# Attention stage: reciprocal denominators carried through memory, a convolution tap on ScalarE and POOL, and new ranks in the plan

## The chip, the cores and the metric

The program runs on one core of one Trainium2 chip. A core has TensorE (PE, with its weight loads PEld), VectorE (DVE), ScalarE (ACT), GpSimd (POOL) and SyncE (SP, which here only issues transfers). The metric is the device time of one execution in microseconds; the median of three runs before the change is 3934.19 us.

## The reference

Two layers act on `x` of shape (32, 1024, 14, 14), in float32. Layer 0 (group normalisation and three table-lookup convolutions) is untouched by the change. Layer 1 is linear attention with a rotary embedding and a depthwise 3 x 3 convolution:

```python
q = elu(q_pre) + 1;  k = elu(k_pre) + 1            # q_pre, k_pre: 1x1 products over half of the channels each
q_rope, k_rope = rope(q), rope(k)
km = kh.mean(axis=-1)
z = 1.0 / (einsum('bhdn,bhd->bhn', qh, km) + 1e-06)
kv = s * s * einsum('bhdn,bhen->bhde', krh, vh)
out = einsum('bhdn,bhde->bhne', qrh, kv) * z[..., None]
lepe = conv_depthwise_3x3(x, lepe_w) + lepe_b
return attn + lepe                                  # x = x + layer1(group_norm(x))
```

There are 16 heads of 64 channels; an image has 196 positions.

## The kernel before, in words

Layer 0 runs first. When it is done, the attention stage handles 16 **pairs** of images, p = 0 to 15. Channels lie in 8 tiles of 128 partitions; a pair's tile has 2 x 196 = 392 columns. Each pair goes through these steps (the line is that of the instruction in the profile before):

- `load`: SP loads two halves h of four tiles into buffers `x` (L992) and the third convolution's output into `o3q` (L1006), two tiles at a time.
- `front`, `group_norm`, `normalise`: layer 0's last sum (L1023, L1032, L1037), statistics (L1042), averages on PE (L1064), `centred` and `variance` on DVE (L1072 to L1080), a power and small products on POOL (L238 to L1091), and two scaled copies by ACT (L1117): `y`, which is the attention's input with a border, and `x`, to which the middle tap of the convolution is already applied. `y` has two buffers, for even and odd pairs.
- `channels`: the query and key products, 4 matmuls each (L1149), relu and exp on ACT (L1158, L1161), and a maximum on DVE (L1166, L1170). A PE result takes one of 4 banks of the pool `mm`.
- `rope`: four products and sums on POOL for each of 4 key and 4 query tiles (L1190 to L1197).
- `v_tokens`, `k_tokens`, `products`: turns on PE (L1208) with copies by ACT (L1211), then kv on PE (L1245) and a mask on DVE (L1254).
- `normalisers`: means of k (L1278), denominators on PE (L1296), then `z`, the reciprocals, on DVE (L1305, L1306). `z` holds 4 rows in use for each group of 32 partitions.
- `normalise_q`, four times: a matmul with a selection matrix spreads the four rows over 128 partitions (L1317) into a bank of `mm`, ACT copies it into one of two buffers `zb` (L1323), and POOL multiplies the roped query `qr` by it (L1320).
- `attend`, four times, each for two tiles: the product of scaled query and kv into two of three banks `pa` (L1337).
- `lepe`, eight times: the other eight taps of the convolution, each one DVE instruction that adds a shifted and weighted `y` onto the bank (L1354), then the sum into `x` (L1368). `store` writes four tiles of `x` out (L1377).

No loop order sets where an instruction stands. Every step calls `do(engine, rank, weight, fn, reads, writes)`, which records a piece; `Plan.write` then plays all 16 pairs on paper, with the weights as durations. Each time an engine is free on paper, it is given the ready piece with the lowest rank for which buffers are free, and the real instruction is emitted then. On the chip each engine executes its own list in that order and waits where the real dependencies aren't met. A rank is a due time: pair p starts at t = 80 p, and `attend` and `lepe` of pair p have ranks over t + 80, so they stand among the work of pair p + 1. A piece's results count as there after its weight and a `lag` (0.12 for most).

Of the kernel before, what the change touches and what calls it, by code (L numbers as in the profile page):

```python
# [51 lines left out]
class Plan:  # L52
# [31 lines left out]
    def write(self):  # L84
# [29 lines left out]
        while events:  # L114
            now, _, done = heapq.heappop(events)
            if done is not None:
                for m in after[done]:
                    count[m] -= 1
                    if count[m] == 0:
                        heapq.heappush(ready[self.pieces[m][0]], (self.pieces[m][1], m))  # L120
                for s in self.pieces[done][5]:
                    s.left -= 1
            if events and events[0][0] <= now:
                continue
            for e in engines:
# [28 lines left out]
                heapq.heappush(events, (now + w, 2, None))  # L154
                heapq.heappush(events, (now + w + lag, 1, piece))
        assert left == 0, [p for p, c in zip(self.pieces, count) if c == 0][:0] or left
# [4 lines left out]
def conv_preact_kernel(ctx: ExitStack, tc: tile.TileContext, a: dict, out: bass.AP):  # L161
# [692 lines left out]
    with ExitStack() as s:  # L854
# [99 lines left out]
        bufs = dict(x=5, o3q=2, e=2, k=2, q=4, qr=5, ks=2, zb=2, mm=4, pa=3, w=1)  # L954
# [95 lines left out]
        def group_norm(p, h, rank):  # L1050
# [19 lines left out]
            def centred():  # L1070
                for t in (g("gd"), pd()):
                    nc.vector.tensor_tensor(t, mean, bc(pm()[:, :8], 2, 2), ALU.subtract)  # L1072
                nc.vector.tensor_tensor(g("gd"), g("gd"), pd(), ALU.mult)
                nc.vector.scalar_tensor_tensor(
                    g("gq"), m2, 1.0 / 98.0, g("gd"), ALU.mult, ALU.add
# [31 lines left out]
        def normalise(p, h, c, xt, rank):  # L1107
# [29 lines left out]
            do(ACT, rank + 24, 0.92, apply("xsc", "xbi", "x"), [key("xsc"), key("xbi")], [xk])  # L1137


        def channels(p, keys, j, r, t, sums, rank):  # L1140
# [35 lines left out]
            do(PE, rank, 2.76, product, ys_, [pq], lag=0.25)  # L1176
# [25 lines left out]
        def tokens(dst, dk, blocks, keys, rank):  # L1202
# [7 lines left out]
            do(PE, rank, 0.5, turn, keys, [pt], lag=0.25)  # L1210
# [12 lines left out]
        def k_tokens(p, i, h, jp, kt, rank):  # L1223
            tokens(
                lambda: kt()[:, jp],
                (kt, jp),
                lambda: [krs[2 * jp + j][:, r, i, h] for j in range(2) for r in range(2)],
                [("kr", 2 * jp + j) for j in range(2)],
                rank,
            )  # L1230
# [42 lines left out]
        def normalisers(qs, ks, rank):  # L1273
# [33 lines left out]

            qk = [(q, r) for q in qs for r in range(2)]
            do(PE, rank, 2.3, piece, [*qk, ("kmm", 0), ("kmm", 1)], [pd], lag=0.25)
            do(DVE, rank - 10, 3.0, inverse, [pd], ["z"])  # L1310

        def normalise_q(j, qr, rank):
            pz, zb = bank("mm"), slot("zb", [P, N2])
            v = slice(32 * j, 32 * j + 32)

            def spread():
                nc.tensor.matmul(pz()[:, :N2], sel[v], z[v], start=True, stop=True)  # L1317
# [4 lines left out]
            do(PE, rank, 0.6, spread, ["z"], [pz], lag=0.25)  # L1322
            do(ACT, rank - 10, 0.48, lambda: nc.scalar.copy(zb(), pz()[:, :N2]), [pz], [zb])  # L1323
            do(POOL, rank, 1.65, times, [zb], [qr], port=True)

        def attend(j, kvs, qr, rank):


            pa = [bank("pa") for hp in range(2)]
# [17 lines left out]

        def lepe(p, c, pa, xt, rank):


            def tap(k):
                def piece():
# [3 lines left out]
                        neighbours(p, c, 15 * (k // 3 - 1) + k % 3 - 1),  # L1356
# [13 lines left out]
            for n, k in enumerate([k for k in range(9) if k != 4]):  # L1370
# [14 lines left out]

        ru = once.tile([P, 2, N2], F32, tag="ru", name="ru")
        z = once.tile([P, N2], F32, tag="z", name="z")

        def pair(p, t):

            xts = {}
            for h in (1, 0):
                f = t - T + (20 if h else 50)
                xts[h], os = load(p, h, f)
                for c in range(4):
                    front(p, h, c, xts[h], os[c // 2], f + 6.5 * c)
                group_norm(p, h, f + 16)
                for c in range(4):
                    normalise(p, h, c, xts[h], f + 40 + c)
# [4 lines left out]
            for j in range(4):  # L1404
                k = slot("k", [P, 2, N2])
                for r in range(2):
                    channels(p, True, j, r, k, ks, t + 9 * j)
                kr = krs[j].rearrange("p r i h (n m) -> p (r i) (h n) m", m=15)[:, :, :, :14]
                rope(k, lambda kr=kr: kr, ("kr", j), j, t + 8 * j + 28)
            for j in range(4):  # L1410
                q, qr = slot("q", [P, 2, N2]), slot("qr", [P, 2, N2])
                for r in range(2):
                    channels(p, False, j, r, q, None, t + 22 + 8.0 * j + 3.0 * r)
                qv = lambda qr=qr: qr().rearrange("p r (i n m) -> p (r i) n m", i=2, m=14)
                rope(q, qv, qr, j, t + 34 + 9 * j + 26)
# [3 lines left out]
            for i in range(2):  # L1419
                for half in (1, 0):  # L1420
                    for h in range(2):
                        v_tokens(p, i, h, half, vts[i][h], t + (22 - 2.0 * half + 3 * h if i == 0 else 66 + h - 2 * half))
# [93 lines left out]
```

## Time and profile before

| | us |
|---|---|
| median of 3 runs (lowest, highest) | 3934.19 (3933.69, 3940.51) |
| the profiled execution, own time | 3939.01 |
| its span | 3937.2 |
| first product of the attention stage | about 2727 |
| start of the 1st, 15th and 16th reciprocal of `z` | 2789.7, 3805.6, 3876.4 |
| busy over the whole span: PE, DVE, POOL, ACT | 3750.7, 3058.5, 2225.9, 1705.0 |

The profile is of one execution. Its views used below are the table by windows (busy time of each engine in a stretch), the timeline of an engine (start, length, engine, line, operation, output and inputs, how many were merged, and in brackets the idle time before it and what ended it), the view of waits (who waited for whom: total us, times, longest), and the groups of instructions by line (busy us and mean ns of one). The mean of a group includes the part of an instruction that overlaps its successor. A matmul of float32 stands in the records as two rows, so one query or key product of 4 matmuls is 8 rows.

### The profile page before, as it was taken

Reading aid. Unit: us, or ns where it says so; the run is one execution under the profiler, and the core shown is the slowest. Engines: PE = TensorE matmul, PEld = TensorE weight load, DVE = VectorE, ACT = ScalarE, POOL = GpSimd, SP = SyncE. Lnnn points to the kernel's source line nnn. Section 1 sums busy time; section 2 is a strip of 40 time slices with the busy share of each in tenths; the row PEclk is TensorE's granted clock in tenths of the full one; section 3 lists DMA queues with packets and bytes.
Section 4 is the critical chain, followed back from the end, with each engine's and each line's share of the span. In section 5 each row is a group of like instructions: output and inputs, shape, how many; then the busy total and the mean of one; then the engine's idle time right before and its main releaser. Section 6 shows DMA issues by size and latency. Waiting matters only on the chain. (4 is left out here: it accounts for less than half of the span.)

```text
span 3937.2 us, 43888 instructions
## 1 busy us (share of the span) xinstructions
PE 3750.7 (95%) x15451; PEld 2172.6 (55%) x15451; DVE 3058.5 (78%) x4391; ACT 1705.0 (43%) x3797; POOL 2225.9 (57%) x1246
## 2 busy tenths in 40 slices
PE   8999999999999999999999999994999999999995
PEld 5555555545555555555444444442666666666664
DVE  8999999977888888888533333323799999999997
ACT  4554555533333333333222111213756666666661
POOL 7999999964444444444211111103877777777773
PEclk9999999998999999999999999997999999999997
DMA  3111111024454444544111100114122222222211
GB/s 113 33 34 33 33 33 33 1 65 83 74 70 72 69 66 71 73 71 64 38 38 38 38 26 31 38 38 135 42 63 66 70 70 64 64 70 69 60 54 33
DMA packets 202085, 220.19 MB, mean 56 GB/s; under 512 B 21048, under 2 KB 199736, under 8 KB 201856
## 3 DMA queue, kind: packets, MB, share of 16 engines
q1 hardware_dynamic: 201280, 217.15, 24.3%
q8 instruction: 124, 2.03, 0.2%
q14 instruction: 105, 0.86, 0.1%
q10 hardware_dynamic: 576, 0.15, 0.0%
HBM read 158.47 MB, written 58.79 MB: 55 GB/s over the span
## 5 line engine op out<-in xcount | busy, mean ns | idle before, releaser
L471 POOL TENSOR_TENSOR t<-t,r 128x1664 f32<-128x1664 f32 (+1 forms) x284 | 1063.9, 3746 | 1205.0 <-DVE r L470 1172.8
L504 PE MATMUL po<-t,lut 128*128 128x392 f32 x4096 | 1406.7, 497 | 0.5 <-POOL t L471 0.5
L504 PEld LDWEIGHTS po<-t,lut 128*128 128x128 f32 x4096 | 770.4, 190 | 594.0 <-issue 57.0
L433 ACT ACTIVATE t<-sc,cbias 128x392 f32<-128x392 f32 (+1 forms) x1136 | 620.6, 592 | 989.4 <-PE sc L722 584.7
L1149 PE MATMUL mm<-y,qk 128*128 128x392 f32 x2048 | 730.2, 509 | 4.1 <-POOL xbi L1091 4.1
L445 DVE STREAM_TRANSPOSE tt<-t 128x1664 f32<-128x1664 f32 (+1 forms) x284 | 544.5, 1917 | 183.0 <-ACT t L433 183.0
L808 PE MATMUL po<-t,lut 128*128 128x448 f32 x1792 | 680.3, 540 | 0.0
L1354 DVE SCALAR_TENSOR_TENSOR pa<-y,lepe_w,pa 128x406 f32<-128x406 f32 x1024 | 605.7, 635 | 10.5 <-PE pa L1337 9.3
L470 DVE STREAM_TRANSPOSE r<-rc 128x1664 f32<-128x1664 f32 (+1 forms) x284 | 546.6, 1925 | 20.6
L1149 PEld LDWEIGHTS mm<-y,qk 128*128 128x128 f32 x2048 | 387.8, 195 | 285.8 <-issue 36.2
L808 PEld LDWEIGHTS po<-t,lut 128*128 128x128 f32 x1792 | 338.4, 190 | 339.9 <-issue 339.6
L817 DVE BATCH_NORM_STATS2 stats<-o 128x6 f32<-128x448 f32 x112 | 68.9, 617 | 488.4 <-ACT o L816 488.4
L462 DVE TENSOR_REDUCE sm<-tt 128x104 f32<-128x832 f32 (+2 forms) x284 | 423.1, 1490 | 5.4
L722 PE MATMUL sc<-patch,cw 72*128 72x392 f32 x1024 | 365.8, 499 | 13.2 <-DMA patch<-h1d 10.1
L722 PEld LDWEIGHTS sc<-patch,cw 72*128 72x128 f32 x1024 | 195.8, 192 | 162.4 <-issue 21.5
L448 POOL TENSOR_TENSOR tt<-tt 128x832 f32<-128x832 f32 x128 | 247.9, 1937 | 7.8 <-DVE tt L445 7.8
L816 ACT COPY o<-po 128x448 f32<-128x448 f32 x112 | 59.0, 527 | 419.6 <-PE po L808 375.5
L464 DVE RECIPROCAL rc<-sm 128x104 f32<-128x104 f32 (+1 forms) x284 | 229.4, 808 | 9.8
L1190 POOL TENSOR_TENSOR kr<-k,cosq 128x784 f32<-128x784 f32 x64 | 104.1, 1627 | 132.8 <-DVE k L1170 107.4
L1320 POOL TENSOR_TENSOR qr<-qr,zb 128x784 f32<-128x784 f32 x64 | 116.0, 1844 | 103.7 <-ACT zb L1323 103.7
L472 ACT ACTIVATE sm<-sm 128x104 f32<-128x104 f32 (+1 forms) x284 | 82.9, 292 | 174.9 <-DVE rc L464 174.8
L1023 ACT ACTIVATE w<-x,tb,gn_a 128x196 f32<-128x196 f32 x256 | 133.3, 521 | 58.5 <-DMA x<-in_x_dram 34.0
(140 smaller groups left out, 3677.1 us busy)
## 6 DMA issues: line engine op xcount, KB each, us to landing
patch<-h1d SPq DMA_DIRECT2D x567, 108.5 KB
x<-in_x_dram SPq DMA_DIRECT2D x32, 784.0 KB
o3d<-o SPq DMA_DIRECT2D x14, 1792.0 KB
x<-in_x_dram SPq DMA_DIRECT2D x64, 392.0 KB
o3q<-o3d SPq DMA_DIRECT2D x64, 392.0 KB
out_dram<-x SPq DMA_DIRECT2D x64, 392.0 KB
lut<-in_lut_dram SPq DMA_DIRECT2D x24, 512.0 KB
h1d<-pad SPq DMA_DIRECT2D x32, 225.0 KB
```

What stands on the lines that cost most here:

```text
L433: nc.scalar.activation(t[:, j, : sc.shape[1]], sc, AF.Identity if exact else AF.Exp, bias=bias[:, j : j + 1],)
L445: nc.vector.transpose(tt, tf)
L448: nc.gpsimd.tensor_tensor(tv[:, :, :8], tv[:, :, :8], tv[:, :, 8:], ALU.add)
L462: nc.vector.tensor_reduce(sm, tv, AX.X, ALU.add)
L464: nc.vector.reciprocal(rc, sm)
L470: nc.vector.transpose(r, bc(rc, 2, KC))
L471: nc.gpsimd.tensor_tensor(tf, tf, r, ALU.mult)
L504: nc.tensor.matmul(po[h], luts[b][:, j, h * P : (h + 1) * P], ts[u % len(ts)][:, j, :N2], start=(b == 0 and j == 0), stop=(b == 7 and j == 3),
L722: nc.tensor.matmul(sc, w2[:, 4 * b + j, :], pv[:, 4 * (b % 2) + j, :, :14, :14], start=True, stop=True,)
L808: nc.tensor.matmul(po, luts[g][:, m * P : (m + 1) * P], t3[h][:, g % 4, :], start=(g == 0), stop=(g == 7),)
L1149: nc.tensor.matmul(pv(), w[kt][:, m0 : m0 + P], ywin(p, first + kt), start=(kt == 0), stop=(kt == 3),)
L1354: nc.vector.scalar_tensor_tensor(acc, neighbours(p, c, 15 * (k // 3 - 1) + k % 3 - 1), lw[:, c, k : k + 1], acc, ALU.mult, ALU.add,)
```

## The change

1. For pairs 0 to 14, `normalisers` writes `z` to a DRAM tile `zd` (two of them, for even and odd pairs) by a transfer on SP, and `normalise_q` reads each group's four rows back with a broadcast source, 32 times each, into one of now four buffers `zb`. The plan gives the write a lag of 2.5 and the reads of 5.0, 6.7, 8.4 and 10.1. Pair 15 keeps the matmul and the ACT copy.
2. In `lepe`, for tiles 4 to 7 one tap, and in pair 15 three taps of every tile, are taken from DVE: ACT multiplies the shifted window of `y` by the weight into a buffer `side` (of two), and POOL adds it onto `x`.
3. `centred` puts its squared difference into the bank and not into `gd`.
4. In the plan, a piece releases pieces of its own engine (other than SP) at once, without the lag. A key product of the next pair waits for the turns of this pair's keys (`held`), and a turn waits until its target buffer has room (`room`).
5. Nearly all ranks have new values, from a table `due`. In pair 15 the denominators have a lower rank, and every second `attend` takes its banks from `mm`.

The instructions of PE in steady pairs are the same apart from the spread's matmuls, which are left only in pair 15; their order changes. In a steady pair, PE has after the denominators: one turn, two key products of the next pair, two kv products, two more key products, an average of group normalisation, and then the first `attend`.

```diff
         while events:
-            now, _, done = heapq.heappop(events)
+            now, kind, done = heapq.heappop(events)
             if done is not None:
                 for m in after[done]:
-                    count[m] -= 1
-                    if count[m] == 0:
-                        heapq.heappush(ready[self.pieces[m][0]], (self.pieces[m][1], m))
-                for s in self.pieces[done][5]:
+                    own = self.pieces[m][0] == self.pieces[done][0] != "SP"
+                    if own == (kind == 0):
+                        count[m] -= 1
+                        if count[m] == 0:
+                            heapq.heappush(ready[self.pieces[m][0]], (self.pieces[m][1], m))
+                for s in self.pieces[done][5] if kind else ():
                     s.left -= 1
...
-                heapq.heappush(events, (now + w, 2, None))
+                heapq.heappush(events, (now + w, 0, piece))
                 heapq.heappush(events, (now + w + lag, 1, piece))
...
-        bufs = dict(x=5, o3q=2, e=2, k=2, q=4, qr=5, ks=2, zb=2, mm=4, pa=3, w=1)
+        bufs = dict(x=5, o3q=2, e=2, k=2, q=4, qr=5, ks=2, zb=4, side=2, mm=4, pa=3, w=1)
...
-                nc.vector.tensor_tensor(g("gd"), g("gd"), pd(), ALU.mult)
+                nc.vector.tensor_tensor(pd(), g("gd"), pd(), ALU.mult)
                 nc.vector.scalar_tensor_tensor(
-                    g("gq"), m2, 1.0 / 98.0, g("gd"), ALU.mult, ALU.add
+                    g("gq"), m2, 1.0 / 98.0, pd(), ALU.mult, ALU.add
                 )
...
-            do(PE, rank, 2.76, product, ys_, [pq], lag=0.25)
+            held = [("held", j // 2)] if keys else []
+            do(PE, rank, 2.76, product, ys_, [pq, *held], lag=0.25)
...
-            do(PE, rank, 0.5, turn, keys, [pt], lag=0.25)
+            do(PE, rank, 0.5, turn, keys, [pt, (dk[0], "room")], lag=0.25)
...
-                [("kr", 2 * jp + j) for j in range(2)],
+                [("kr", 2 * jp + j) for j in range(2)] + [("held", jp)],
...
+            def keep():
+                nc.sync.dma_start(zd[p % 2], z)
...
             do(DVE, rank - 10, 3.0, inverse, [pd], ["z"])
+            if p < NP - 1:
+                do(SP, rank - 10, 0.45, keep, ["z"], [("zd", p % 2)], lag=2.5)
...
             def spread():
+                nc.sync.dma_start(zb(), bc(zd[p % 2, 32 * j : 32 * j + 4], 1, 32))
+
+            def select():
                 nc.tensor.matmul(pz()[:, :N2], sel[v], z[v], start=True, stop=True)
...
-            do(PE, rank, 0.6, spread, ["z"], [pz], lag=0.25)
-            do(ACT, rank - 10, 0.48, lambda: nc.scalar.copy(zb(), pz()[:, :N2]), [pz], [zb])
+            if p < NP - 1:
+                do(SP, rank - 10, 0.58, spread, [("zd", p % 2)], [zb], lag=5.0 + 1.7 * n)
+            else:
+                do(PE, rank, 0.6, select, ["z"], [pz], lag=0.25)
+                do(ACT, rank - 10, 0.48, lambda: nc.scalar.copy(zb(), pz()[:, :N2]), [pz], [zb])
             do(POOL, rank, 1.65, times, [zb], [qr], port=True)
...
-            for n, k in enumerate([k for k in range(9) if k != 4]):
+            taps = [k for k in range(9) if k != 4]
+            last = p == NP - 1
+            shared = 3 if last else c // 4
...
+            def apart(k):
+                side = slot("side", [P, 2, 14, 14])
+
+                def shifted():
+                    nc.scalar.activation(
+                        side(), window(offset(k)), AF.Copy, scale=lw[:, c, k : k + 1]
+                    )
+
+                def onto():
+                    nc.gpsimd.tensor_tensor(
+                        xc(), xc(), side().rearrange("p i r c -> p (i r c)"), ALU.add
+                    )
+
+                do(ACT, rank - 6, 0.52, shifted, [("y", p % 2, c)], [side])
+                do(POOL, rank - 4, 1.02, onto, [side], [(xt, c % 4)], port=True)
+
+            for k in range(shared):
+                apart(taps.pop(1))
+            for n, k in enumerate(taps):
                 do(DVE, rank + n, 0.555, tap(k), [("y", p % 2, c)], [pa])
...
-            normalisers(qs, ks, t + 68)
+            normalisers(p, qs, ks, at["den"] - (10 if p == NP - 1 else 0))
...
+                pool = "mm" if p == NP - 1 and n % 2 else "pa"
+                pa = attend(j, kvs, qrs[j], pool, at["attend"] + due["sums"] * n)
```

Some of the new ranks, beside the old ones for a pair at t: the key product of tile j stood at t + 9 j and stands at t + 10.25 j; the denominators at t + 68, now t + 69; `normalise_q` at t + 70, now t + 64; `attend` number n at t + 82.5 + 19 n, now t + 82.5 + 20 n; the fronts of the halves began at t - 60 and t - 30 and begin at t - 72 and t - 28.

## The prediction

> **What bounds the kernel now.** The edits lie in the attention stage alone, so I read the tenths of part 2 only to place it (about 2697 us to the end) and then the stage by itself. First the table by windows, over twelve whole periods from one reciprocal to the same one twelve pairs on (2934.89 to 3805.60), with the columns PE, PEld, DVE, ACT, POOL, clock, DMA share, GB/s:
>
> ```profile
> 2934.89:3805.60 870.71, 856.24 (x5286) 578.04 (x5282) 833.72 (x1961) 570.60 (x1196) 642.02 (x576) 0.97 0.23 67
> ```
>
> Divided by 12: a pair takes 72.56 us, in which PE is busy 71.4, DVE 69.5, POOL 53.5, ACT 47.6. PE and DVE are both nearly full, and a busy PE here may be a PE that waits inside a group of matmuls. So next PE's timeline over a period, at the place where the reciprocal is used:
>
> ```profile
> 3589.64 2.39 PE L1317 MATMUL mm<-z,hsel 32*128 32x392 f32 x8 [0.99 <-DVE z L1306]
> 3591.96 7.23 PE L1149 MATMUL mm<-y,qk 128*128 128x392 f32 x16
> ...
> 3601.51 10.78 PE L1149 MATMUL mm<-y,qk 128*128 128x392 f32 x32
> ...
> 3662.00 2.78 PE L1317 MATMUL mm<-z,hsel 32*128 32x392 f32 x8 [0.99 <-DVE z L1306]
> 3664.71 8.48 PE L1149 MATMUL mm<-y,qk 128*128 128x392 f32 x16
> ```
>
> PE idles 0.99 us for the reciprocal, spreads it for 2.3 to 2.7, and then 16 matmuls take 7.1 to 8.3 us from start to the next group's start, where 32 take 10.6 (0.332 each, so 16 should take 5.3). These 16 wait for banks. The view of waits (2867 to 3767) says who holds them:
>
> ```profile
> POOL qr L1320 <- ACT zb L1323: 81.3, 12, 8.1
> ACT zb L1323 <- PE mm L1317: 57.8, 12, 5.1
> ACT zb L1323 <- POOL qr L1320: 25.2, 25, 1.6
> PE mm L1317 <- DVE z L1306: 11.6, 12, 1.1
> ```
>
> The four spreads fill all four banks of `mm`; ScalarE may copy the third and fourth out only when POOL (1.84 us each) has given back one of two `zb` buffers. So a knot of 0.99 + 2.32 + 1.8 = 5.1 us (period of 72.4) or 0.99 + 2.71 + 3.0 = 6.7 us (period of 74.0) stands in every pair, and **without it both periods come to 67.3 us**. DVE is just behind, and its largest row is the taps:
>
> ```profile
> L1354 DVE SCALAR_TENSOR_TENSOR pa<-y,lepe_w,pa 128x406 f32<-128x406 f32 x767 | 457.4, 635 | 0.8
> L1074 DVE SCALAR_TENSOR_TENSOR gq<-gst,gd 128x16 f32<-128x16 f32 x24 | 10.8, 449 | 0.8
> ```
>
> The 635 ns includes what overlaps the next one; seven in a row take 3.92, so one costs 0.555. The second row is small but odd: the same 16 columns cost 172 ns in its neighbours. The timelines show why:
>
> ```profile
> 3600.07 0.18 DVE L1074 SCALAR_TENSOR_TENSOR gq<-gst,gd 128x16 f32<-128x16 f32 x1
> 3635.13 0.65 DVE L1074 SCALAR_TENSOR_TENSOR gq<-gst,gd 128x16 f32<-128x16 f32 x1
> ```
>
> ```profile
> 3634.22 1.53 POOL L1191 TENSOR_TENSOR ru<-q,sinq 128x784 f32<-128x784 f32 x1
> ```
>
> The slow one ends when POOL's instruction ends (3635.75). Last, the end, from DVE's timeline (the bracket is the idle before):
>
> ```profile
> 3885.68 8.86 DVE L1354 SCALAR_TENSOR_TENSOR pa<-y,lepe_w,pa 128x406 f32<-128x406 f32 x16 [2.65 <-PE pa L1337]
> ...
> 3897.60 8.95 DVE L1354 SCALAR_TENSOR_TENSOR pa<-y,lepe_w,pa 128x406 f32<-128x406 f32 x16 [2.12 <-PE pa L1337]
> ```
>
> The last pair's taps bound the end: four times 16 taps, and before each DVE waits for PE, since two of three `pa` banks must be free first.
>
> [...]
>
> **The change, part by part** (for one pair of the first 15, unless said).
>
> *Spread through memory.* Gone: 4 matmuls and 4 copies of ScalarE, and with them the whole knot, since no bank is held and `zb` has four buffers: PE 72.56 to 67.3. Added: a write of 200 KB and four reads. SP issues five more DMAs at 0.37 to 0.47 us, 2 us a pair beside about 5; the reads wait in SP for the write's landing, and behind them stand the next o3q load, a store and the x loads. PE and DVE waited for no load in the waits of twelve pairs[...].
> Is the trip covered? In the new order of instructions PE has, between the denominators (1.5 us) and the first product that needs a scaled query: a turn 0.44, two key products 5.3, the second image's two kv products 3.65 together, two more key products 5.3 and an average 0.45, in all 15.1 at the durations of PE's timeline. So the attend stands 16.6 us after the denominators begin. The trip: 1.5, then add and reciprocal 0.56 + 2.6[...], POOL 1.84[...].[...] **Worth -5.26 us a pair of PE time**, with both ends: all of it[...].
>
> *One tap in half the tiles.* DVE loses 4 of 64 taps: 4 x 0.555 = 2.2 us. ScalarE gets 4 of 0.55 (nearest L1161, 530, and L1158, 580 ns) for 4 copies of 0.485: unchanged at 47.9. POOL gets 4 additions of 128x392 like L1194 (951 to 1027 ns): 53.5 to 57.6 us. `added` waits for that addition; POOL's plan puts it a few us ahead, and half the tiles don't have one.
>
> *centred.* gq reads PSUM and one SBUF input: 2 x (449 - 172) = 0.55 us of DVE. DVE: 69.5 - 2.2 - 0.55 = 66.7 us.
>
> *Ranks, held, room, same-engine releases.* They change the order only. No row shows what an order costs: between -1 and +2 us a pair; I take +0.5, because two engines at 67.3 and 66.7 that feed each other's banks can't both be full all the time (now PE loses under 0.5 us outside the knot).
>
> So a pair goes to **67.8 us, -4.75**. Over the 14 periods between the first reciprocal (2789.7) and the fifteenth (3805.6): -66 us.
>
> *Last pair.* It keeps the spread on PE. 24 taps leave DVE, 24 x 0.555 = 13.3; every second attend uses `mm` banks, so the three waits of 2.12 should go, 6.4; the knot behind the 15th reciprocal goes, 5.3. Against it POOL gets 24 additions of 1.02, 24.5 us, and at 58 us busy in the last 131.6 it has room, but the ropes and scalings queue behind them: give back 3.5. Sum -21.5 (between -10 and -28).
>
> *Start of the stage.* New ranks in the first 93 us: taken at nothing, -5 to +5: the first pair waits for its loads and statistics whatever the ranks.
>
> Sum: -66 - 21.5 = -88 us against the profiled execution, whose own time is 3939.0 (span 3937.2, 1.8 around it): 3851. The median of the runs shown, 3934.2, lies 4.8 lower, so **3846 us**.
>
> **Rivals.**
> (A) *The trip is longer than its cover, or PE and DVE interlock worse.* 2.5 us a pair come back, a period of 70.3: 14 x 2.26 = 32, tail 18, so 3884. For it: shape (4 rows) and write-then-read are nowhere in the trace, and POOL stands in order behind the first read. Against it: [...]DMA share only 0.23.
> (B) *POOL becomes the bound; slower.* POOL idles 19 us a pair now, waiting for keys, queries and `zb`. In the new order it stands before the first scaling until the read lands, with the next pair's key ropes behind it, on which k tokens, kv and attend hang. If its 19 us of waits can't shrink, a pair takes 57.6 + 19 = 76.6: 14 x 4.0 = +57, tail -15, 3976. It decides from 15 us of waits on (72.56 - 57.6). Against it: 81.3 / 12 = 6.8 us of the 19 are the wait for the first copied `zb`, and the rest waits for keys and queries that PE delivers sooner when the knot is gone; nothing says that their sum is fixed.
> (C) *No change.* The new order makes a knot of the same size at another place, PE waiting for banks that a late DVE gives back, and the tail's 24 POOL additions hold up the end by as much as the taps gave: all 88 us returned, 3934. It needs 5 us a pair more than PE loses outside the knot now; little speaks for it.
> That the edits don't do what they say is excluded by the order of instructions: the spread's matmuls are left in the last pair only.
>
> **Numbers.** Forecast (period 67 to 68.8) 0.63, A 0.24, C 0.04, B 0.09. The forecast's ends: 14 x 5.5 + 28 + 5 = -110, 3824, and with the plan 1 us worse 3860; at DVE's own sum of 66.7 a pair, 14 x 5.86 + 28 + 5 = 115, 3819; above, A is taken in up to 3893. Faster by over 0.2% (8 us, about what a measurement can tell): 0.88; within: 0.03; slower: 0.09.
>
> **What would show it.** Right: the spread's matmuls 8 rows in all (L1317 has 8 a pair); no group of 16 products over 5.5 us after the reciprocal; period 67 to 69; DVE about 66.7 a pair; gq near 172 ns; POOL near 57.6. Wrong: PE's attend waiting for POOL's scaling and that for a DMA (A), or PE waiting for kr or qr with POOL still idle for about 19 us a pair (B); the tail after the last reciprocal still over 55 us (60.8 now).

## The result, and the profile after

The changed kernel takes **3973.57 us** (median of four runs, 3970.85 to 3974.95), against 3934.78 before (also of four): ratio 1.0095, 95% interval 1.0077 to 1.0112. It is slower, where the prediction had it 88 us faster. The span of the profiled execution is 3969.1 us, 31.9 above that of before. Where these lie, by the start of the reciprocal (L1306 before, L1311 after):

| profiled execution | before, us | after, us | difference |
|---|---|---|---|
| start to the 3rd reciprocal | 2934.9 | 2945.8 | +10.9 |
| 3rd to 15th reciprocal, 12 pairs | 870.7 | 898.5 | +27.8 |
| 15th reciprocal to the end | 131.6 | 124.8 | -6.8 |

First the table by windows of the kernel after, over the same twelve pairs (stretch, its length, then busy us and count of PE, PEld, DVE, ACT and POOL, clock, DMA share, GB/s):

```profile
2945.83:3844.30 898.47, 829.16 (x5184) 564.54 (x5183) 862.38 (x1922) 588.31 (x1200) 688.29 (x624) 0.99 0.25 78
```

A pair takes 74.87 us and not 72.56. PE fell from 71.4 to 69.1 us a pair, as the spreads left it and its clock rose from 0.97 to 0.99; DVE, from which the change takes four taps, **rose** from 69.5 to 71.9. It is DVE that is nearly full now. POOL is at 57.4.

The place of the old knot, in the timeline of all engines after:

```profile
3613.97 1.53 PE L1301 MATMUL mm<-q,kmm 128*32 128x196 f32 x32
3615.96 5.43 PE L1152 MATMUL mm<-y,qk 128*128 128x392 f32 x16
3618.46 2.60 DVE L1311 RECIPROCAL z<-z 128x392 f32<-128x392 f32 x1
3621.09 0.34 SPq L1314 DMA_DIRECT2D zd<-z  x1
3621.32 3.71 PE L1250 MATMUL mm<-vt,kt 105*64 105x128 f32 x64
3623.04 2.34 SPq L1330 DMA_DIRECT2D zb<-zd  x4
3624.96 5.53 PE L1152 MATMUL mm<-y,qk 128*128 128x392 f32 x16
3629.38 1.84 POOL L1336 TENSOR_TENSOR qr<-qr,zb 128x784 f32<-128x784 f32 x1
3632.50 3.06 PE L1356 MATMUL pa<-qr,kv 64*128 64x210 f32 x16
```

The knot is gone: PE works while the reciprocals go out and come back, and 16 rows of products take 5.4 to 5.5 us where they took 7.2 to 8.5. The trip is covered: the write is issued 0.03 us after the reciprocal, SP goes on to the reads 1.95 us later, POOL's first scaling begins another 6.3 us on and didn't wait for a read, and the attend begins 18.5 us after the denominators. How long write and read would take was the author's estimate; the nearest wait in before, that of an `x` load for a store, was 4.7 us at most. The view of waits (2867 to 3767; who waited for whom, total us, times, longest) agrees, and has PE's and ScalarE's new waits for DVE:

```profile
ACT w L1026 <- DVE x L1040: 54.9, 35, 2.9
PE mm L1152 <- ACT kt L1216: 16.0, 11, 1.5
PE mm L1067 <- DVE gst L1045: 14.8, 12, 1.5
PE mm L1152 <- DVE k L1173: 13.2, 11, 2.3
PE mm L1067 <- DVE nmc L1080: 12.7, 18, 0.9
POOL qr L1336 <- DMA zb<-zd: 1.6, 3, 1.2
```

POOL waited 1.6 us for the reads in all, and no knot of 57.8 and 81.3 us is left. Instead PE waits some 40 us for three results of DVE (`gst`, `k` and `nmc`). What DVE does with its time, by groups in the same stretch (busy us, mean ns of one):

```profile
L1375 DVE SCALAR_TENSOR_TENSOR pa<-y,lepe_w,pa 128x406 f32<-128x406 f32 x722 | 462.5, 641 | 16.5
L1283 DVE TENSOR_TENSOR kmm<-ks,hmean 128x32 f32<-128x32 f32 x26 | 13.9, 544 | 0.0
L1077 DVE SCALAR_TENSOR_TENSOR gq<-gst,mm 128x16 f32<-128x16 f32 x24 | 4.2, 174 | 0.8
```

`gq` went from 453 to 174 ns, as predicted; that an input from the bank would do this was the author's estimate. The taps' mean says nothing, since it counts the overlap. DVE's timeline does: these are the longest runs of taps, two of after and one of before.

```profile
3594.14 4.72 DVE L1375 SCALAR_TENSOR_TENSOR pa<-y,lepe_w,pa 128x406 f32<-128x406 f32 x7
3636.44 4.72 DVE L1375 SCALAR_TENSOR_TENSOR pa<-y,lepe_w,pa 128x406 f32<-128x406 f32 x7
```

```profile
3636.93 4.46 DVE L1354 SCALAR_TENSOR_TENSOR pa<-y,lepe_w,pa 128x406 f32<-128x406 f32 x8
```

Seven taps took 4.72 us and eight took 4.46. With 0.64 for the last one, a step from tap to tap is (4.72 - 0.64) / 6 = **0.68 us after, (4.46 - 0.63) / 7 = 0.55 before**. Counted in the two lists of DVE's instructions, 695 of 940 taps after are followed at once by an instruction that uses the same bank, most of them the next tap of the same tile; before it was 58 of 1024. Each such tap adds onto the bank that its predecessor has just added onto, and starts some 0.04 us after that one's recorded end (0.64 us long), where one on another bank starts 0.08 us ahead of it (0.63). Whether it waits for that result or for the bank as such was not separated: in these kernels the two go together.

At the end, the runs of taps of the last pair:

```profile
3932.26 3.37 DVE L1375 SCALAR_TENSOR_TENSOR pa<-y,lepe_w,pa 128x406 f32<-128x406 f32 x5 [6.85 <-PE pa L1356]
3936.15 3.36 DVE L1375 SCALAR_TENSOR_TENSOR pa<-y,lepe_w,pa 128x406 f32<-128x406 f32 x5
```

Five taps of one tile follow each other at 0.68, a quarter more than 0.55. Behind the sixteenth reciprocal the 24 taps taken away and the freed banks show all the same: 46.3 us to the end, where it was 60.8. But from the fifteenth to the sixteenth it takes 78.6 us and not 70.8, and so 6.8 of the forecast 21.5 us are left.

### The profile page after: what moved, and what is told of

Its sections match the earlier page's. It is cut to its first block, busy times and chain, and to the rows that moved or that the text cites. A ratio compares the mean times of both kernels' runs of the same rounds, so it can differ in the third digit from the quotient of the medians.

```text
span 3969.1 us, 43744 instructions
## 1 busy us (share of the span) xinstructions
PE 3717.1 (94%) x15331; PEld 2153.9 (54%) x15331; DVE 3077.2 (78%) x4307; ACT 1738.3 (44%) x3821; POOL 2307.8 (58%) x1330
## 5 line engine op out<-in xcount | busy, mean ns | idle before, releaser
L1152 PE MATMUL mm<-y,qk 128*128 128x392 f32 x2048 | 710.9, 499 | 38.3 <-ACT kt L1216 17.9
L1375 DVE SCALAR_TENSOR_TENSOR pa<-y,lepe_w,pa 128x406 f32<-128x406 f32 x920 | 589.6, 641 | 28.4 <-PE pa L1356 6.9
L725 PE MATMUL sc<-patch,cw 72*128 72x392 f32 x1024 | 366.2, 500 | 11.2 <-DMA patch<-h1d 9.5
L1161 ACT ACTIVATE e<-mm,kbd 128x392 f32<-128x392 f32 x128 | 74.0, 578 | 181.7 <-PE mm L1152 181.5
```

The source lines that it names most:

```text
L725: nc.tensor.matmul(sc, w2[:, 4 * b + j, :], pv[:, 4 * (b % 2) + j, :, :14, :14], start=True, stop=True,)
L1152: nc.tensor.matmul(pv(), w[kt][:, m0 : m0 + P], ywin(p, first + kt), start=(kt == 0), stop=(kt == 3),)
L1375: nc.vector.scalar_tensor_tensor(acc, neighbours(p, c, offset(k)), lw[:, c, k : k + 1], acc, ALU.mult, ALU.add,)
```

## Experiments

**Theory 1**: the plan's new release rule (an own engine's next piece is ready at once) puts taps of one bank back to back, and the rest of the change does what the prediction said. **Theory 2** (rival): the trip, the tap or the new ranks cost what was gained, and the rule is harmless. All ratios are to the kernel before, run on the same chip beside it.

### The release rule

**e1.** The whole change, with the old rule:

```diff
-                    own = self.pieces[m][0] == self.pieces[done][0] != "SP"
-                    if own == (kind == 0):
-                        count[m] -= 1
...
+                    count[m] -= 1
...
-                heapq.heappush(events, (now + w, 0, piece))
+                heapq.heappush(events, (now + w, 2, None))
```

> The changed kernel with the plan's release rule of before (a result counts for its own engine after the lag of 0.12 too); all else as changed. In the order of instructions, taps followed at once by a user of the same bank fall from 695 to 68 of 940. Theory 1 (DVE waits about 0.125 us for its own result whenever a tap follows a tap of the same bank): tap to tap 0.55 us again, DVE near 67 us a pair, period 68 to 69, time 3845 to 3870 us. Theory 2 (the new ranks, POOL's additions or the trip through memory cost the time): within 15 us of 3973.

3910.25 us, ratio 0.9935 (0.9919 to 0.9952): between the two expectations, so each was only half right. The rule costs 63 us of the changed kernel. What is left is a gain of 26, and not of 88. Its window line (12 pairs) and a run of its taps:

```profile
2934.68:3798.20 863.52, 826.40 (x5186) 555.05 (x5185) 808.92 (x1921) 582.00 (x1201) 688.75 (x625) 0.99 0.28 82
```

```profile
3598.51 5.58 DVE L1372 SCALAR_TENSOR_TENSOR pa<-y,lepe_w,pa 128x406 f32<-128x406 f32 x10
```

Ten taps in 5.58 us are steps of 0.55 again (68 of 940 taps stand ahead of a user of their bank), and DVE is busy 67.4 us a pair, where the prediction had 66.7. A pair takes 71.96.

**e2.** The kernel before, with nothing but the new rule (the same lines, the other way round).

> The kernel before with the new release rule alone. Taps followed at once by a user of the same bank rise from 58 to 763 of 1024. Theory 1: 705 x 0.125 = 88 us more for DVE, 5.5 a pair, so DVE would need 75 where a period is 72.6: period 75 to 77, time 3970 to 4000 us. Theory 2: within 10 us of 3934.

4022.47 us, 1.0219 (1.0202 to 1.0236): 86 us for a rule that neither adds nor removes an instruction. 763 of 1024 taps stand ahead of a user of their bank, and over twelve pairs:

```profile
2945.44:3884.26 938.82, 874.40 (x5286) 583.94 (x5284) 902.41 (x1969) 587.34 (x1202) 642.20 (x576) 0.96 0.21 62
```

DVE goes from 69.5 to 75.2 us a pair (902.41 / 12), and the pair from 72.6 to 78.2, by as much. 705 more such taps at 0.13 us are 92 us in 16 pairs, 5.7 a pair. The time is more than the 3970 to 4000 us that were expected. The rule reorders the other engines too, so this run alone doesn't show that all of it is DVE's.

**e3.** The change with its new rule, but the taps of two tiles recorded together, so that two banks alternate:

```diff
-            for n, k in enumerate(taps):
-                do(DVE, rank + n, 0.555, tap(k), [("y", p % 2, c)], [pa])
+            for n, (k, (fn0, c0, pa0)) in enumerate(zip(taps, first)):
+                def both(fn0=fn0, fn1=tap(k)):
+                    fn0()
+                    fn1()
...
+                do(DVE, rank - due["taps"] + 2 * n, 1.11, both, ks_, [pa0, pa])
```

> The changed kernel, its new release rule kept, with one plan piece for a tap of both tiles of an attend, so that taps of two banks alternate (no tap is followed by a user of its own bank). Theory 1: tap to tap 0.55 us, time 3845 to 3880 us. Theory 2: within 15 us of 3973. If it is the release rule for some other instructions than the taps: between 3900 and 3960.

3904.69 us, 0.9919 (0.9903 to 0.9936). The rule stays, no tap stands ahead of a user of its bank, DVE is at 67.5 us a pair and the loss against e1 is gone. The time lies above the range of theory 1, as e1's does, and in the one that was kept for other instructions than the taps. What speaks for the taps all the same is that nothing is left of the 63 us, though the edit changes the taps' ranks too. So it is the neighbourhood of the taps, not the rule as such. A run of its taps, for comparison with the seven in 4.72:

```profile
3611.12 4.46 DVE L1375 SCALAR_TENSOR_TENSOR pa<-y,lepe_w,pa 128x406 f32<-128x406 f32 x8
```

**e8.** The change, with the old rule for DVE alone and the new one for PE, ScalarE and POOL:

```diff
-                    own = self.pieces[m][0] == self.pieces[done][0] != "SP"
+                    own = self.pieces[m][0] == self.pieces[done][0] not in ("SP", "DVE")
```

> The changed kernel with the release rule of before for DVE alone; PE, ScalarE and POOL keep the new one. If all of the rule's cost is DVE's waiting for its own results: within 10 us of e1_old_release (3910). If dependent instructions in a row on POOL or ScalarE cost as well: 3925 to 3960.

3935.54 us, 0.9991 (0.9982 to 0.9999). So 38 of the 63 us are DVE's, and 25 come with the rule on the other three engines: 10 in the twelve pairs (72.8 against 71.96 a pair) and 15 behind the fifteenth reciprocal, where the stretch to the sixteenth takes 81.5 us and not 58.1. The changed kernel ends only 2 us later than e8 behind the fifteenth, so most of its lost end is this part of the rule and not its slow taps. Where on these engines the time goes was not traced (POOL's busy time is that of e1, 57.4 us a pair); that e3, which keeps the rule there, loses nothing suggests that it hangs on the order as a whole.

### The knot: what each edit is worth alone, and what the knot was

**e5.** The kernel before with the trip through memory alone; old ranks, old rule.

> The kernel before with the trip of the reciprocals through memory alone (zb four buffers, the plan's lags for the transfers), its ranks and release rule as before. If the knot of my prediction is what bounds a pair: PE 67.3, DVE 69.5 a pair, so DVE is next and a period comes to 69.5 to 70.5: 3885 to 3905 us. If an order of instructions loses elsewhere what the knot gives: 3915 to 3940.

3937.90 us, 0.9998 (0.9989 to 1.0007): nothing. **e6**, the tap by ScalarE and POOL and `centred` alone:

> The kernel before with the taps on ScalarE and POOL and the change in centred alone; spread on PE, ranks and release rule as before. The knot stays, so a period stays near 72.5, and only the last pair gains: 3915 to 3930 us. If POOL's additions hold up the chain through POOL: above 3940.

3929.86 us, 0.9980 (0.9970 to 0.9990). **e7**, both, still with old ranks and rule:

> The kernel before with the trip, the taps and centred; ranks and release rule as before, no held and room. If what e1_old_release lacks of my forecast is the new ranks' fault: 3850 to 3880 us. If two nearly full engines lose it in any order: 3895 to 3920.

3906.42 us, 0.9919 (0.9902 to 0.9935). The windows of the three over twelve pairs, in the order e5, e6, e7:

```profile
2932.90:3810.65 877.75, 828.76 (x5190) 556.98 (x5188) 860.08 (x1969) 559.45 (x1153) 641.74 (x576) 0.99 0.27 81
```

```profile
2932.48:3805.87 873.39, 857.12 (x5284) 579.16 (x5282) 810.47 (x1921) 599.00 (x1248) 690.43 (x624) 0.97 0.23 67
```

```profile
2925.39:3782.71 857.32, 817.58 (x5190) 555.84 (x5188) 818.01 (x1925) 587.30 (x1202) 689.43 (x624) 1.00 0.28 83
```

Divided by 12: with the trip alone DVE is busy 71.7 of 73.1 us; with the taps alone PE 71.4 of 72.8; with both PE 68.1 and DVE 68.2 of 71.4. Two engines were nearly full, so that each edit alone only showed the other one: by the ratios 1 and 8 us cheaper alone, and 32 together. e7 lies within 4 us of e1 (6 by the ratios), so the new ranks, with `held` and `room`, are neither the fault nor a gain on the whole.

That DVE **rose** in e5, from 69.5 to 71.7, has a cause of its own: two small groups of instructions take longer. First before, then e5 (its `gq` took 453 ns before):

```profile
L1278 DVE TENSOR_TENSOR kmm<-ks,hmean 128x32 f32<-128x32 f32 x24 | 6.0, 248 | 0.0
```

```profile
L1074 DVE SCALAR_TENSOR_TENSOR gq<-gst,gd 128x16 f32<-128x16 f32 x25 | 25.8, 1032 | 0.9
L1278 DVE TENSOR_TENSOR kmm<-ks,hmean 128x32 f32<-128x32 f32 x24 | 23.7, 1002 | 0.0
```

Of the 24 `kmm` in this stretch of e5, 23 took over 0.5 us, and each of these ended 46 to 60 ns after an instruction of POOL, as if it waited for that one. The two groups cost 2.7 us a pair more than before. With `centred`, `gq` stays short (175 ns in e7), which beside the trip is worth 1.8 us a pair and not 0.55; that is part of what the two edits gain only together.

The trip wasn't hidden from POOL everywhere: in these twelve pairs POOL waited for the reads 19.9 us in e1, 8.7 in e7 and 55.0 in e5 (in four waits of 13 to 14 us for the most part). PE hardly felt it: its waits for the scaled `qr` are 3.5 us in e7, the most of the three.

**e4.** e1 (the change, old rule), with the spread on PE for all pairs.

> As e1_old_release, and the spread of the reciprocals on PE with copies by ScalarE for all 16 pairs as before, no trip through memory (zb has four buffers). Theory 1 with the knot of my prediction: PE's 3.3 to 5 us a pair come back, period 71 to 73, time 3900 to 3930. If the trip through memory is worth nothing or costs: at or below e1_old_release.

3974.16 us, 1.0095 (1.0079 to 1.0112). The trip is worth 64 us there, against 5.26 x 14 = 74 in the prediction. The range of the expectation was missed because it stood on that of e1, 3845 to 3870; the distance of some 55 to 60 us between the two was about right.

**e13.** What was the stall of 1.8 to 3.0 us behind the spread? The prediction read "banks", held because only two `zb` were free. The kernel before, with four:

```diff
-                lambda: (space or p2).tile(shape, F32, tag=pool, name=pool, bufs=bufs[pool]),
+                lambda: (space or p2).tile(shape, F32, tag=pool, name=pool, bufs=4 if pool == "zb" else bufs[pool]),
```

> The kernel before with four buffers zb in memory where it had two (the plan still counts two, so that the order stays). In before the 16 products behind the spread take 7.2 to 8.5 us where 16 take 5.3 elsewhere. Reading of the prediction: the four banks of mm are held because ScalarE may copy the third and fourth spread only when POOL has freed a zb. Then this kernel frees them at once and a pair gains 1.5 to 3 us: about 3890 to 3915. Rival: the records show PE's granted clock at 0.50 for 3.3 or 6.7 us just there, and every matmul at half speed; then the banks have nothing to do with it and nothing changes: 3930 to 3940, the clock still 0.50 behind the spread.

3938.77 us, 1.0001 (0.9991 to 1.0010). ScalarE's wait for POOL's `zb` (25.2 us in 12 pairs before) is gone from the view of waits, and PE's timeline has not moved:

```profile
3589.31 2.39 PE L1317 MATMUL mm<-z,hsel 32*128 32x392 f32 x8 [0.99 <-DVE z L1306]
3591.63 7.23 PE L1149 MATMUL mm<-y,qk 128*128 128x392 f32 x16
```

**So it was not the two `zb`**, and what the prediction says of the 16 products, "These 16 wait for banks", doesn't hold. The column of the clock, in windows of 3.4 us around two knots of the kernel before, says what it was (PE busy is the number behind the first comma, the clock the third from the right):

```profile
3588.20:3591.60 3.40, 2.32 (x18) 1.12 (x12) 3.40 (x6) 1.03 (x3) 0.47 (x1) 1.00 0.00 0
3591.60:3595.10 3.50, 3.50 (x7) 1.68 (x6) 3.50 (x9) 1.56 (x4) 3.50 (x3) 0.58 0.23 46
```

```profile
3660.40:3663.80 3.40, 2.31 (x19) 1.27 (x16) 3.40 (x5) 0.88 (x3) 0.31 (x1) 1.00 0.00 0
3663.80:3670.60 6.80, 6.80 (x11) 3.19 (x10) 5.03 (x12) 2.17 (x5) 6.80 (x4) 0.50 0.22 61
```

Behind a stretch in which PE was busy 2.3 of 3.4 us, the granted clock stands at half for about 3.4 or 6.8 us (0.50 from 3592.2 to 3595.6 and from 3663.9 to 3670.7, by windows of 0.5 us). Half speed for 3.4 us costs 1.7, for 6.8 us 3.4: the rows of 16 that took 7.23 and 8.48 us and not 5.5. In both stretches PE had idled 0.99 us in one piece for the reciprocal. That PE's busy time alone decides is not so: in the changed kernel PE idled 1.80 us in one piece, and the clock stayed full in this stretch and the next (1.00 in both).

```profile
2956.70:2960.10 3.40, 1.60 (x13) 0.97 (x13) 3.37 (x10) 1.12 (x2) 3.40 (x4) 1.00 0.32 105
```

What decides whether the clock falls behind such idle time stays open.

**e16.** The test of whether the gap brings the fall: the kernel before, with four products more, ahead of the first spread and into its bank, so that PE has work while the reciprocals are made (the main lines of the edit):

```diff
             def spread():
+                for k in range(0 if n else 4):
+                    nc.tensor.matmul(
+                        pz()[:, :N2], wq[0][:, :P], ywin(p, 0), start=True, stop=True
+                    )
                 nc.tensor.matmul(pz()[:, :N2], sel[v], z[v], start=True, stop=True)
```

> The kernel before with four extra products (128x392, 0.332 us each, 1.33 us together) into the bank of the first spread, ahead of it: PE has work while it would idle 0.99 us for the reciprocal. They leave the output as it was. If the slow stretch behind the spread is only bank waits: 0.34 us a pair more, about 3940. If the clock is halved because PE idled in the stretch before, the filler keeps it: 1.7 to 3.3 us a pair less than before in most pairs, minus 0.34: 3890 to 3920, and the clock of the stage goes from 0.97 to 0.99 or 1.00. In between if four are too few.

3927.91 us, 0.9971 (0.9965 to 0.9978). The filler is eight rows and took 2.90 us a pair, twice what the expectation put (a matmul is two rows). With all that useless work the kernel is 11 us **faster**:

```profile
3653.12 2.90 PE L1318 MATMUL mm<-y,qk 128*128 128x392 f32 x8
3655.96 0.94 PE L1321 MATMUL mm<-z,hsel 32*128 32x392 f32 x8
3657.45 2.90 PE L1149 MATMUL mm<-y,qk 128*128 128x392 f32 x8 [0.56 <-ACT zb L1327]
```

```profile
3652.90:3656.30 3.40, 3.40 (x18) 1.79 (x18) 3.40 (x6) 0.00 (x0) 0.00 (x0) 1.00 0.00 0
3656.30:3659.70 3.40, 2.84 (x15) 1.40 (x8) 1.82 (x5) 2.16 (x5) 2.22 (x2) 1.00 0.00 0
```

The clock is 1.00 in every pair, the spreads take 0.94 and not 2.4 to 3.1, and a pair 71.6 us (859.32 / 12). Without filler, spread and the wait of 0.56 that is 71.6 - 2.90 - 0.94 - 0.56 = 67.2: the prediction's 67.3 us of work for PE hold, though of the 5.3 us that stood in their way some 2 were the clock (0.97 over 72.6 us before).

### The 3.6 us that stay open: 71.4 and not 67.8

**e10** and **e11** take work away from e7 in the same order of instructions: e10 one tap in tiles 0 to 3 of pairs 0 to 14, e11 the fourth matmul of one of two query products.

```diff
# e10
+                none = not shared and n == 1
-                do(DVE, rank + n, 0.555, tap(k), [("y", p % 2, c)], [pa])
+                do(DVE, rank + n, 0.555, (lambda: None) if none else tap(k), [("y", p % 2, c)], [pa])
# e11
-                for kt in range(4):
+                last = 2 if r and not keys else 3
+                for kt in range(last + 1):
```

> e7_trip_and_taps_old_ranks with one tap left out in each of tiles 0 to 3 of pairs 0 to 14 (the output lacks these taps), the plan's order the same: DVE 2.2 us a pair less. If DVE alone bounds e7: period 71.4 to 69.2, 3873. If PE alone does: unchanged, 3906. If the two, in lockstep by the order, share it: in between, 3885 to 3898.

> e7_trip_and_taps_old_ranks with the fourth matmul left out of one of the two query products of each j (the queries lack a quarter of their sum there), the plan's order the same: PE 4 x 0.66 = 2.6 us a pair less. If PE alone bounds e7: 3866. If DVE alone: unchanged. If both share it: 3880 to 3898.

e10: 3900.41 us, 0.9901 (0.9886 to 0.9916), 6 below e7; a pair takes 70.4, so 1.1 of the 2.2 us of DVE came through (12.7 us in twelve pairs, of which the two ends give back most). e11: 3918.61, 0.9951 (0.9935 to 0.9966), 12 **above** e7. It has 8 rows, 2.7 us, less for PE in a pair, and the clock gives it back:

```profile
3557.80:3561.30 3.50, 1.91 (x9) 1.04 (x7) 3.50 (x8) 1.60 (x4) 3.42 (x4) 1.00 0.56 171
3561.30:3568.20 6.90, 6.42 (x46) 5.95 (x48) 4.97 (x9) 6.14 (x14) 5.13 (x8) 0.52 0.00 0
```

Its mean clock over twelve pairs is 0.97 where e7 has 1.00; of 72.1 us a pair, that is 2.2. Less work made more idle time (2.07 us in one piece, up to 3561.8), and behind it PE ran at half clock (0.52).

**e9.** e7, with the means `kmm` as eight instructions of one tensor input and a weight, not two of two inputs (and in the plan 0.35 for 0.2, without the lock that keeps POOL away):

> e7_trip_and_taps_old_ranks with the means of k (two DVE products with two SBUF inputs a pair) written as eight small ones with a pointer scalar, so one SBUF input. If these two wait for POOL (DVE spends 4.1 us a pair on this line group in e7 and 2.7 before): DVE loses about 1 us a pair, and the time falls by 5 to 15 us below 3906. If their waits are hidden: within 4 us of 3906.

3964.43 us, 1.0069 (1.0056 to 1.0083), 58 above e7. The eight are no shorter together: 612 ns each on average for 8 columns, 4.3 us a pair where the two took 1.8. Without the lock, the plan now puts them beside POOL's work, and the trace shows what that does:

```profile
3208.59 6.22 DVE L1279 TENSOR_SCALAR kmm<-ks,hmean 128x8 f32<-128x8 f32 x8
3209.57 1.02 POOL L1194 TENSOR_TENSOR qr<-qr,ru 128x392 f32<-128x392 f32 x1
3210.54 1.53 POOL L1190 TENSOR_TENSOR qr<-q,cosq 128x784 f32<-128x784 f32 x1
```

Over twelve pairs 33 of the 96 took longer than 0.3 us, and each of the 33 ended 28 to 37 ns after an instruction of POOL; none of the 63 short ones (some 0.22 us) lies within one. By that the long ones wait for POOL as well, one of its instructions each, and nothing else runs on DVE in the 6.22 us of the eight above. Every second pair takes 77.4 us, and in it PE first stands for DVE's `gq`, which comes behind the eight, and then has half the clock.

```profile
3216.53 1.02 PE L1064 MATMUL mm<-gq,gavg 128*128 128x8 f32 x4 [4.39 <-DVE gq L1074]
```

```profile
3215.20:3222.00 6.80, 5.47 (x14) 3.83 (x15) 6.73 (x19) 0.59 (x1) 3.00 (x4) 0.52 0.17 54
```

**e12** and **e14** add the change's two edits of the last pair (denominators 10 earlier, banks of `mm` for every second attend), e12 to e9, e14 to e7:

```diff
-            normalisers(p, qs, ks, t + 68)
+            normalisers(p, qs, ks, t + 68 - (10 if p == NP - 1 else 0))
...
+                pool = "mm" if p == NP - 1 and n % 2 else "pa"
```

> e9_means_one_input with the last pair's edits of the change (denominators ten earlier, every second attend in mm banks). The stretch from the 15th reciprocal to the end was 12 us shorter in e1_old_release, which has them, than in e7, which has not: 10 to 14 us below e9, about 3885 and below all kernels so far. If those 12 us were the new ranks': no different from e9.

> The kernel with both computing edits, old ranks and old release rule (3906.4), with the change's two edits of the last pair added: its denominators 10 earlier in the plan, banks of mm for every second attend. With old ranks the time from the fifteenth reciprocal to the end was 11.3 us shorter than before, with the whole change under the old rule 23.6. If these two edits make that difference: 3892 to 3898. If it lies in the ranks: 3902 to 3908.

e12: 3960.12 us, 1.0056 (1.0042 to 1.0069); e14: 3905.94, 0.9920 (0.9903 to 0.9936). They bring 4 and 0 us: by elimination, the shorter end of e1 is a matter of its ranks (or of `held` and `room`).

**e15.** e14, with one tap by ScalarE and POOL in all eight tiles (`shared = 3 if last else 1`).

> The last kernel with one tap by ScalarE and Pool in all eight tiles of a pair instead of four (the last pair as it was). DVE 68.2 to 66.0 us a pair, POOL 57.5 to 61.5, ScalarE the same within 0.5. Leaving these four taps out altogether gave 6 us. If POOL's extra work hides: 6 to 12 us below the last kernel. If POOL, which keys and queries pass in order, becomes late: equal to it or up to 15 above.

3907.71 us, 0.9928 (0.9911 to 0.9945): nothing. DVE falls to 64.7 us a pair and POOL rises to 61.2; a pair takes 71.2. Leaving the same taps out gave 1.1, so the additions on POOL give it back, or the order does.

**e17** and **e18** ask who holds PE in e7. Its waits over twelve pairs:

```profile
PE mm L1149 <- ACT vt L1211: 15.4, 12, 1.7
PE mm L1208 <- ACT vt L1211: 6.6, 8, 1.5
PE mm L1208 <- DVE kv L1254: 5.6, 9, 1.0
PE pa L1351 <- DVE x L1384: 4.6, 5, 1.4
```

No wait is large. Most are for ScalarE's copies of turned tokens, which stand in ScalarE's list behind a `y` that waits for POOL (45.3 us in 12 pairs; before 0.2) or a `w` that waits for DVE (35.5; before 6.1). e17 tells the plan that POOL's coefficients come 4 us later; e18 ranks the copies 50 earlier:

```diff
# e17
-                POOL, rank, 1.9, scale, [key("gve"), key("nmc")], [key("ga"), key("gb")], port=True
+                POOL, rank, 1.9, scale, [key("gve"), key("nmc")], [key("ga"), key("gb")], port=True,
+                lag=4.0,
# e18
-            do(ACT, rank - 10, 0.49, lambda: nc.scalar.copy(dst(), pt()[:TP]), [pt], [dk])
+            do(ACT, rank - 60, 0.49, lambda: nc.scalar.copy(dst(), pt()[:TP]), [pt], [dk])
```

> The kernel with both computing edits, old ranks and old release rule (3906.4), with one number of the plan changed: the group norm's coefficients from POOL count as ready 4 us later, so that ScalarE is given other work ahead of the y that needs them. There ScalarE waits 45 us in 12 pairs for them and 36 for DVE's x, with the token copies behind it, and PE 24 us for these copies (before: 0.2, 6 and 1). If PE's idle time comes from ScalarE's queue standing at y: that wait under 20 us, PE's wait for copies under 15, and a pair 0.7 to 1.5 us shorter: 3888 to 3898. If the idle time only moves (y late for the products instead): 3900 to 3912.

> The same kernel with the plan's rank of ScalarE's token copies 50 earlier, so that they pass every other work of ScalarE that is ready with them. If PE's 24 us of waits for copies are a matter of ScalarE's order: under 12 us, and a pair up to 1 us shorter, 3893 to 3902. If the copies wait because an instruction already ahead of them stands in the queue for another engine: no change within 5 us, 3901 to 3911.

e17: 3917.62 us, 0.9950 (0.9934 to 0.9967), worse than either branch. The wait for the coefficients is gone altogether, but ScalarE's for DVE's `x` rose to 48.3 and DVE's for PE's `pa` from 14.6 to 35.7: the idle time moved. e18: **3901.70 us, 0.9910 (0.9893 to 0.9926)**, 5 below e7, with PE's waits for copies of `vt` halved (22.0 to 11.2) and a pair at 70.7. It is the fastest complete version measured, 34 us below the kernel before and 72 below the change as it was made, though its interval overlaps those of e3 and e7.

## Why the prediction was wrong, by its own steps

| step | predicted | measured |
|---|---|---|
| knot gone, PE's work | 67.3 us a pair | 67.2 (from e16) |
| reason of the stall behind the spread | banks, `zb` | half clock (e13, e16) |
| trip covered | all of the 5.26 us (its length an estimate) | PE waited for the scaled `qr` 1.8 us in 12 pairs, POOL for the reads 1.6 (e1: 0.5 and 19.9) |
| taps and `centred`, DVE | 66.7 us a pair | 67.4 (e1), 71.9 with the rule |
| POOL, ScalarE | 57.6, 47.9 | 57.4, 49.0 |
| **ranks, held, room, same-engine releases** | **+0.5 (-1 to +2)** | **+4.7 (e1, the old rule), +7.6 with the rule** |
| end (15th reciprocal on) | -21.5 | -23.8 (e1), -6.8 with the rule |
| start (to the 1st reciprocal) | 0 (-5 to +5) | -2.2 (e1), +19.3 with the rule (10.9 are left at the 3rd) |

**The step that failed is "Ranks, held, room, same-engine releases. They change the order only".** It priced an order at +0.5 us a pair and took every instruction's duration as fixed. Two things were wrong in it.

*The release rule.* A tap's 0.555 us was taken from a run of before in which taps of two banks alternate. That is a price of a neighbourhood, not of an instruction. The old rule's lag of 0.12, which looks like slack, is what kept a tap and its successor on the same bank apart: while it ran, the plan took a ready piece of another bank. With the rule, 695 taps stand ahead of a user of their bank, at 0.13 each. The rule costs 63 us, of which 38 go with its use on DVE (e8): 35 of the 63 in the twelve pairs, where DVE has 4.5 us more a pair, and the rest at the start and the end. The diff has it in four lines, and comparing the two lists of DVE's instructions would have shown the new neighbours before any run. A neighbour on another bank starts 0.55 us after a tap that runs 0.63; one on the same bank starts 0.13 later, at 0.68.

*The interlock.* Without the rule a pair takes 71.4 (e7) to 72.0 us (e1), and not 67.8. The prediction named the mechanism (two engines near 67 that feed each other's banks) and sized it from PE's loss outside the knot, under 0.5 us. But that was measured while the knot gave every other engine 5 us of slack in each pair. With the knot gone ScalarE's list, which serves both, stands where it never stood before. The term is 4.1 to 4.7 us, 3.6 to 4.2 above the 0.5 that it was given. e10, e15, e17 and e18 moved it by 0.2 to 1.1 us each (e17 the wrong way). One part has a name: `kmm`, whose long ones end just behind POOL's instructions, 1.8 us of DVE a pair in e7 and 0.5 before. Otherwise no single wait carries it. Taking work from one engine alone (e10, e11) gave half of it or nothing; what the least possible is was not shown, and why the term is as large as it is stays open.

What was right: the trip hides from PE, and `centred` gives `gq` the time that was forecast. With the old rule the end shortens by about the forecast sum, but that is partly luck: e1 gains 12.7 us ahead of the sixteenth reciprocal (forecast 5.3) and 11.0 behind it (forecast 16.2). Of the rivals, B gave 3976 us, 2 from the result, by another mechanism: its sign was PE waiting for POOL's `kr` or `qr`, and PE waits 1.8 us for these in twelve pairs; e1, with the same work for POOL, takes 63 us less. A (interlock, 3884, up to 3893) was nearest to the change without its rule, 3910.

## What to carry to other kernels

Before an order is called free, look at what stands next to what on each engine: here a chain of accumulations onto one bank cost 0.68 us a step back to back (after) and 0.55 with another bank's in between (e3), and a planner's lag between dependent pieces can be what interleaves them (the lag of 0.12: 68 such neighbours in e1, 695 without it). Where two engines are nearly full, price an edit by what the other engine leaves, and don't size their interlock from a kernel in which a stall gave both slack. Read the clock's column beside every stretch of PE that is slower than its like: here idle time cost twice, once as idle (0.99 us) and once as half clock behind it (0.50 for 3.4 or 6.8 us), and useless work of 2.9 us a pair paid (e16, 11 us).

## What the runs showed of the hardware, not expected

- A DVE instruction of 406 columns that adds onto the bank of the one ahead of it starts 0.68 us after it, and 0.55 us after one of another bank (after against e3).
- The granted clock of PE fell to half for about 3.4 or 6.8 us behind 3.4 us in which PE was busy 1.9 to 2.3 (before, e11), but not behind one in which it was busy 1.60 (after): busy time alone doesn't tell. Filling the gap with 2.9 us of useless products a pair made the kernel 11 us faster.
- Small DVE instructions grow where the order puts them beside POOL's: the means with two tensor inputs from 248 ns in before to 894 in e7, and those with a single tensor input and a weight took 612 ns on average for 8 columns (e9). The long ones of both kinds end within 60 ns after an instruction of POOL (e5, e7, e9), which is what a wait for that instruction looks like.
